# Layer 2 of a decoder on one core: self attention with halves of heads, norms in steps, and an MLP in a written order

## The chip, the cores and the metric

The kernel runs on one core of a Trainium2 chip. A core has a matrix engine (PE, whose weight loads the profile shows as PEld), a vector engine (DVE), an activation engine (ACT), a general engine (POOL), and SP, whose queue starts DMAs. Data lies in SBUF (128 partitions); matmuls write to PSUM, eight banks of 128 x 512 float32. The metric is device time of one execution in microseconds, lower is better; the figure given for the kernel is the median of five.

## The reference, cut to what matters

x is 8 sequences of 112 tokens of width 256 (the functions carry other default sizes; the shapes of the inputs rule). Twelve sublayers follow each other, each added to x. The change is in two of them, the first two of layer 2:

```
x = x + L2_attn(layernorm(x))
x = x + L2_xattn(layernorm(x), ctx_512)

L2_attn:   q = h @ Wq (8 heads of 128), k, v = h @ Wk, h @ Wv (4 heads of 128, each for two q heads)
           q, k = q*cos + rotate_half(q)*sin, the same for k     # rotate_half: (-second half, first half)
           softmax(q k^T / sqrt(128) with a causal mask) @ v, heads side by side, @ Wo
L2_xattn:  x = ln(xx; ln1);  x = x + mha(x, x; a1)               # causal mask after the softmax
           x = ln(x; ln2);   return x + mha(x, ctx; a2)
  mha(x, y): o = softmax(q k^T / sqrt(32)) v, 16 heads of 32, of ln(x), ln(y)
             x_out = x + o @ li1 + b;  return x_out + gelu(ln(x_out) @ li2 + b) @ li3 + b
```

The context ctx_512 has 375 tokens of width 128 for each sequence.

## The kernel before, in words

All is float32 unless said. x stays in SBUF as [token, sequence, width]. T = 896 tokens are worked on in two halves of HT = 448 (four sequences each). Weights come in blobs of up to 1 MB through a ring of eight tiles (`_Ring`, L330 to L352): SP loads the next blob when `done` says that a tile is dead. The program is written through a framework that finds dependences, allocates tiles (a pool's tag with bufs buffers; a new pool takes the space of a closed one, so its tiles wait for the old ones) and orders the instructions of each engine by trace order and readiness. Inside `manual_schedule` PE, DVE and ACT keep the written order among that region's instructions; where they fall among others stays free.

`normalise` (L451) takes `stats` (L433: bn_stats and bn_aggr of each sequence, L440, L441), `rsqrt` (L413: ten small DVE instructions, L418 to L430) and one DVE instruction a sequence (L454). `turned` (L473) transposes four sequences of 128 columns on PE (L477). `mm` (L407) issues matmuls at L410; `cp` (L399) copies in turn on DVE (L403) and ACT (L405); `add_to_x` adds at L493.

`l2_attn` (L1472) has no written order. For each half it makes eight q chunks and four k chunks of 128 rows (two matmuls of 448 columns, which the profile counts as two instructions each), with the rotation of L1496 (two products on 64 partitions that cross over), L1499 (product with cos) and L1500 (sum, on POOL). Then, for each sequence: v (`value`, one matmul group of 512 columns), and for two groups of four heads scores, `softmax_rows` (mask added L503, maximum L505, subtraction L506, exponential L507), `row_sums` (L1527, L1528), `heads_T` (e transposed, L515), the product with v and its scaling (L1518); `out_T` (L539) turns o, and eight matmuls with wo and an add follow.

`l2_xattn` (L1553) opens x1 and xo. `a1_attend` (L1583) first does norm 1 of half 0 (`affine_norm`, L1531: normalise with a second rsqrt, times gain plus bias at L1538 and L1539, odd sequences on POOL, then normalise into xn), turns it (L1546 applies gain and bias), makes q and k of half 0, then norm 1 of half 1; a written loop over the sequences follows: scores, their maxima (L960), q of half 1, denominators and result of earlier ones, the turned maxima nT (L966, copied on DVE at L1631), k of half 1, exponent (L1642, L1649, L1656; the mask product mT on POOL, L1658), product with v of the sequence before (L977), `value` of the next. `query_key`, `value` and `result` share one PSUM bank, "mm". L1671 is a reciprocal, L1676 the scaled copy oT, L1581 the add to xo.

Then a POOL DMA fetches the context (cx, L1564, rows of 512 bytes from the order [sequence and chunk, 125 tokens]). `mha_mlp` (L1742), without a written order, norms xo, and for each half computes eight chunks of the hidden layer (gelu at L1759), calls `ctx_norm` (L1708: in step 0 the norm of 24 context chunks, in step 1 their turns, L1720, and evictions to yT, L1723), and then the output (L1766 bias on POOL, L1767 add). x1 is added (L1567), and `a2_attend` calls the shared `cross` (from L1098): keys and values of sequence 0 from yT (L1135, L1145), norm 2 and turns of half 0, queries (L1156), norm 2 and turns of half 1, and a written loop (maxima L1174, exponentials L1180, turns L1187).

The first layer's `l0_attend` (from L678) is in the form that the change gives to `l2_attn`: a mask matmul in bfloat16 (L739), scores over 64 rows (L746), negated maxima (L755), exponentials with accumulated sums (L761), division before the turn (L769, L770), turns (L778, L780) and a product that comes out transposed (L786, L792).

The functions that the change touches:

Of the kernel before, what the change touches and what calls it, by code (L numbers as in the profile page):

```python
# [12 lines left out]

# [95 lines left out]

def _down(w):  # L110

    return w.transpose(0, 2, 1).reshape(-1, D)


def _weights(inp):
# [75 lines left out]
    def heads(w):  # L191
# [3 lines left out]
        [("l2a_wq", _fm(a("Wq")))],  # L195
        [("l2a_wk", _fm(a("Wk"))), ("l2a_wv", _fm(a("Wv")))],
# [64 lines left out]
def _constants():  # L261
# [12 lines left out]
    for r in range(16):  # L274
# [10 lines left out]
        ("sin", np.concatenate([sin, -sin])),  # L285
# [21 lines left out]
def _pack(inp):  # L307
# [7 lines left out]
        "in_ctx": np.ascontiguousarray(inp["ctx_512"].reshape(NB * CTX, DC)),  # L315
# [8 lines left out]


# [30 lines left out]
class _Kernel:  # L356
# [56 lines left out]
    def rsqrt(self, var, rows, n):  # L413

        nc, small = self.nc, self.small
        va, r0, w, p, rs = (self.t(small, [P, 24], tag)[:rows, :n] for tag in ("va", "r0", "rw", "rp", "rs"))
        vec = nc.vector
# [4 lines left out]
        vec.tensor_scalar(r0.bitcast(I32), r0.bitcast(I32), -1.0, float(0x5F300000), ALU.mult, ALU.add)  # L422
        root = 0.446405130**0.5
        vec.scalar_tensor_tensor(w, r0, root, va, ALU.mult, ALU.mult)
        vec.tensor_tensor(w, w, r0, ALU.mult)
        vec.scalar_tensor_tensor(p, w, -1.38883461 / root, w, ALU.add, ALU.mult)
        vec.scalar_tensor_tensor(p, p, 1.94247540, r0, ALU.add, ALU.mult)
        vec.scalar_tensor_tensor(w, p, -0.5, va, ALU.mult, ALU.mult)
        vec.tensor_tensor(w, w, p, ALU.mult)
        vec.scalar_tensor_tensor(rs, w, 1.5, p, ALU.add, ALU.mult)  # L430
        return rs

    def stats(self, src, rows, n, twice=False):  # L433
# [5 lines left out]
        for i in range(n):  # L439
            nc.vector.bn_stats(st[:rows, i, :], src[:rows, i, :])  # L440
            nc.vector.bn_aggr(mv[:rows, i, :], st[:rows, i, :])  # L441
        var = mv[:rows, :n, 1]
        rs = self.rsqrt(var, rows, n)
        if twice:
            v2 = self.t(small, [P, 24], "v2")[:rows, :n]
            nc.vector.tensor_tensor(v2, rs, rs, ALU.mult)
            nc.vector.tensor_tensor(v2, v2, var, ALU.mult)
            nc.vector.tensor_tensor(rs, rs, self.rsqrt(v2, rows, n), ALU.mult)
        return mv, rs

    def normalise(self, src, dst, rows=S, n=NB, twice=False):  # L451
        mv, rs = self.stats(src, rows, n, twice)
        for i in range(n):
# [3 lines left out]
            )  # L457

# [6 lines left out]
    def ln_T(self, ps, half=None, tag="tr"):  # L465

        for h in (0, 1) if half is None else (half,):
            bs = slice(h * HB, (h + 1) * HB)
            self.normalise(self.x[:, bs, :], self.xn[:, bs, :], n=HB)
# [26 lines left out]
    def softmax_rows(self, sc, work, heads, scale, mask=None):  # L496

        nc = self.nc
        e = self.t(work, [P, 4, S], "e")[:S, :heads, :]
        mx = self.t(self.small, [P, 4], "mx")[:S, :heads]  # L500
        src = sc
        if mask is not None:
            nc.vector.tensor_tensor(e, sc, mask[:, None, :].to_broadcast([S, heads, S]), ALU.add)  # L503
            src = e
        nc.vector.tensor_reduce(mx, src, AX.X, ALU.max)  # L505
        nc.vector.tensor_tensor(e, src, mx[:, :, None].to_broadcast([S, heads, S]), ALU.subtract)  # L506
        nc.scalar.activation(e, e, AF.Exp, scale=scale)  # L507
        return e

    def heads_T(self, e, work, ps, heads, mask=None):  # L510

        nc = self.nc
        tp = self.t(ps, [P, 512], "tr")
        for j in range(heads):
            nc.tensor.transpose(tp[:S, j * S : (j + 1) * S], e[:, j, :], self.ident[:S, :S])  # L515
        eT = self.t(work, [P, 4, S], "eT")[:S, :heads, :]
        src = tp[:S, : heads * S].rearrange("p (h s) -> p h s", h=heads)
        if mask is None:
            self.cp(eT, src)
        else:  # L520
            nc.vector.tensor_tensor(eT, src, mask[:, None, :].to_broadcast([S, heads, S]), ALU.mult)
        return eT

    def scores(self, ps, qk):
        sc = self.t(ps, [P, 512], "sc")
        for j, (q, k) in enumerate(qk):
            self.mm(sc[:S, j * S : (j + 1) * S], [(q, k)])
        return sc[:S, : len(qk) * S].rearrange("p (h t) -> p h t", h=len(qk))

    def out_T(self, o, work, ps, cols):  # L530

        n = cols // P
        oT = self.t(work, [P, n, S], "oT")
        for c0 in range(0, n, 4):
            m = min(4, n - c0)
            tp = self.t(ps, [P, 512], "tr")
            for j in range(m):
                c = c0 + j
                self.nc.tensor.transpose(  # L539
                    tp[:, j * S : (j + 1) * S], o[:S, c * P : (c + 1) * P], self.ident[:S, :S]  # L540
                )
            self.cp(oT[:, c0 : c0 + m, :], tp[:, : m * S].rearrange("p (c s) -> p c s", c=m))
        return [oT[:, c, :] for c in range(n)]

# [5 lines left out]

    def self_psum(self, ctx):
        return ctx.enter_context(self.tc.tile_pool(name="ps_self", bufs=2, space=PSUM))
# [24 lines left out]
    def ln_T_mm(self, ps, xs):  # L577

        self.normalise(self.x, self.xn)
# [258 lines left out]

    def divided(self, out, av, hd, factor=None):

        nc = self.nc
        n = out.shape[1]
        ri = self.t(self.small, [P, 16], "ri")[:S, :n]
        nc.vector.reciprocal(ri, av[:, :, hd])
        if factor is not None:
            nc.vector.tensor_scalar(ri, ri, factor, None, ALU.mult)
        nc.vector.tensor_tensor(
# [735 lines left out]
    def a1_attend(self, x1, xo, norm):  # L1583
# [9 lines left out]
        with ExitStack() as ctx:  # L1593
# [96 lines left out]
            with tc.manual_schedule(engines={ET.PE, ET.DVE, ET.Activation}):  # L1690
                for b in range(NB):
# [8 lines left out]
                    if b < 4:  # L1700
                        query_key(1, b, 1)
# [533 lines left out]
```

## Time and profile before

| | us |
|---|---|
| median of five runs | 2420.91 |
| the five runs | 2410.22, 2420.80, 2420.91, 2421.53, 2426.51 |
| the profiled execution | 2410.22 |
| its span, first to last instruction | 2408.4 |
| PE, DVE, ACT, POOL busy | 2133.7, 1430.3, 772.9, 216.2 |
| self attention of layer 2, from the last add of the sublayer before to its own last add | 1149.5 to 1295.4 |
| a1: prologue; written loop to the score of sequence 7; to the MLP's first turn | 1295.4; 1322.0; 1409.8 to 1447.2 |
| a1's MLP, to its last matmul; to the first maximum of a2 | 1447.2 to 1509.7; 1531.5 |

Times in a profile run from the span's start. A line of a timeline gives start and duration in us, the engine, the source line, the operation, out<-in with partitions x elements, a count, and in square brackets how long the engine had stood still before it and what ended that. A matmul of float32 counts as two instructions. PEclk is the clock that PE was granted, 1.00 being full.

### The profile page before, as it was taken

How to read it: one execution, taken by the hardware profiler on the slowest of the kernel's cores; microseconds unless marked ns; L12 is line 12 of the kernel's file. 1: busy time of each engine (PE TensorE's matmuls, PEld its weight loads, DVE VectorE, ACT ScalarE, POOL GpSimd, SP SyncE). 2: the span in 40 equal slices, each digit the busy share in tenths (PEclk: the TensorE clock that was granted, in tenths of full speed). 3: DMA queues.
4: the chain of work that ended last, by engine and by line, in shares of the span. 5: the costliest groups of instructions: out<-in, count | busy, mean ns of one | idle time of the engine just before them, and what ended most of it. 6: DMA issues, size and time to landing. Idle time of an engine off the chain costs nothing.

```text
span 2408.4 us, 43235 instructions
## 1 busy us (share of the span) xinstructions
PE 2133.7 (89%) x17032; PEld 1266.6 (53%) x17032; DVE 1430.3 (59%) x3994; ACT 772.9 (32%) x2157; POOL 216.2 (9%) x415
## 2 busy tenths in 40 slices
PE   6999999889898899899898859899999999899944
PEld 3444444455556566546565536466655556556622
DVE  4665566565545567553888557767740123667787
ACT  2333334443211256430111211466321110246522
POOL 0111111000011100000222331100000000100000
PEclk9999999999999999999999989999999999899966
DMA  4000000000100000100001011000111100000000
GB/s 187 2 2 2 2 20 35 30 18 18 53 1 15 19 1 2 36 9 35 36 19 35 19 27 53 19 1 4 68 35 53 52 0 1 1 1 2 2 0 16
DMA packets 10731, 55.94 MB, mean 23 GB/s; under 512 B 1834, under 2 KB 3626, under 8 KB 5793
## 3 DMA queue, kind: packets, MB, share of 16 engines
q1 hardware_dynamic: 8304, 44.57, 5.2%
q0 software_dynamic: 2080, 7.07, 0.9%
q8 instruction: 135, 2.21, 0.4%
q10 hardware_dynamic: 144, 1.54, 0.2%
q14 instruction: 68, 0.55, 0.1%
HBM read 52.23 MB, written 0.92 MB: 22 GB/s over the span
## 4 chain that ended last, share of the span: by engine, by line
PE 67%; DVE 21%; issue 5%; ACT 4%; DMA 1%; POOL 1%; DVEq 0%; ACTq 0%; POOLq 0%
PE mm L410 31%; PE gu L410 6%; PE tr L1187 6%; PE g L649 6%; PE sc L410 4%; PE av L1203 3%; PE tr L410 1%; DVE rot L1496 1%; ACT sg L660 1%; PE av L786 1%; PE av L410 1%; ACT th L671 1%; DVE hT L675 1%; PE s L410 1%; PE g L627 1%
## 5 line engine op out<-in xcount | busy, mean ns | idle before, releaser
L649 PE MATMUL g<-w,hT 128*32 128x256 f32 x3552 | 237.3, 384 | 26.1 <-DVE hT L675 25.9
L1174 DVE TENSOR_REDUCE xnm<-sc 112x1 f32<-112x375 f32 x384 | 184.6, 540 | 28.6 <-PE sc L410 28.0
L1187 PEld LDWEIGHTS tr<-cst,xe 112*125 112x125 f32 x1152 | 151.5, 188 | 94.8 <-issue 37.8
L1187 PE MATMUL tr<-cst,xe 112*125 112x112 f32 x1152 | 192.9, 289 | 7.2 <-DVE xeT L1195 4.3
L410 PE MATMUL mm<-xnT,w 128*128 128x448 f32 x432 | 182.3, 559 | 18.8 <-DVE qT L1499 5.3
L410 PE MATMUL mm<-hT,w 128*128 128x448 f32 x512 | 193.0, 539 | 0.0
L649 PEld LDWEIGHTS g<-w,hT 128*32 128x32 f32 x3552 | 95.4, 109 | 168.1 <-DVE hT L675 124.9
L410 PEld LDWEIGHTS mm<-hT,w 128*128 128x128 f32 x512 | 97.1, 190 | 94.4 <-issue 94.4
L627 PE MATMUL g<-xw,cst 128*32 128x256 f32 x1792 | 138.0, 379 | 0.0
L1195 DVE COPY xeT<-tr 125x336 f32<-125x336 f32 x192 | 97.2, 506 | 67.7 <-PE tr L1187 60.8
L1193 ACT COPY xeT<-tr 125x336 f32<-125x336 f32 x192 | 85.0, 443 | 160.2 <-PE tr L1187 160.2
L410 PEld LDWEIGHTS mm<-xnT,w 128*128 128x128 f32 x432 | 77.8, 192 | 104.0 <-issue 54.0
L1178 ACT ACTIVATE xe<-sc,xnm 112x375 f32<-112x375 f32 x256 | 126.2, 581 | 11.2 <-DVE xnm L1174 11.2
L410 PE MATMUL mm<-w,hT 128*112 128x256 f32 x576 | 129.0, 383 | 0.0
L410 PE MATMUL gu<-xnT,w 128*128 128x448 f32 x320 | 126.1, 549 | 1.6 <-DVE hT L1341 1.2
L410 PE MATMUL mm<-w,oT 128*112 128x256 f32 x416 | 105.8, 405 | 22.2 <-DVE oT L1676 13.8
L410 PEld LDWEIGHTS mm<-w,hT 128*112 128x112 f32 x576 | 102.0, 179 | 25.3 <-issue 3.5
L660 ACT ACTIVATE sg<-g 128x192 f32<-128x192 f32 x224 | 73.9, 330 | 105.3 <-PE g L649 92.8
L671 ACT ACTIVATE th<-cell 128x64 f32<-128x64 f32 x224 | 57.5, 257 | 147.3 <-DVE cell L669 147.0
L410 PEld LDWEIGHTS mm<-w,oT 128*112 128x112 f32 x416 | 74.2, 186 | 52.2 <-DVE oT L1676 15.1
L2089 DVE COPY wq<-tr 128x256 bf16<-128x256 bf16 (+1 forms) x12 | 4.6, 420 | 162.9 <-PE tr L2088 162.9
L673 DVE TENSOR_TENSOR h<-sg,th 128x64 f32<-128x64 f32 x224 | 50.4, 225 | 85.6 <-ACT th L671 85.6
(402 smaller groups left out, 3622.2 us busy)
## 6 DMA issues: line engine op xcount, KB each, us to landing
w<-in_w SPq DMA_DIRECT2D x33, 1024.0 KB, 4.8
raw<-in_wq POOLq DMA_DIRECT2D x3, 1024.0 KB, 5.1
w<-in_w SPq DMA_DIRECT2D x3, 896.0 KB, 6.6
wi<-in_wint POOLq DMA_DIRECT2D x3, 768.0 KB, 6.1
w<-in_w SPq DMA_DIRECT2D x2, 768.0 KB, 4.2
ctxT<-in_ctxT ACTq DMA_DIRECT2D x1, 1500.0 KB, 8.3
cx<-in_ctx POOLq DMA_DIRECT2D x1, 1500.0 KB, 20.9
w<-in_w SPq DMA_DIRECT2D x2, 512.0 KB, 3.5
```

The source lines that it names most:

```text
L410: self.nc.tensor.matmul(out, lhsT, rhs, start=i == 0, stop=i == len(pairs) - 1)
L627: nc.tensor.matmul(g[32 * j : 32 * j + 32, :], pick[:, t % 16, :], xw[:, l, t // 16, 256 * j : 256 * j + 256], start=True, stop=t == 0, sk ...
L649: nc.tensor.matmul(g[32 * j : 32 * j + 32, :], hT[l][:, c, :], whh[l][:, c, 256 * j : 256 * j + 256], start=False, stop=c == 1, skip_group ...
L660: nc.scalar.activation(sg[:, :192], g[:, :192], AF.Sigmoid)
L671: nc.scalar.activation(th, cell[l], AF.Tanh)
L673: nc.vector.tensor_tensor(h, og, th, ALU.mult)
L1174: nc.vector.tensor_reduce(nm, sc, AX.X, ALU.max, negate=True)
L1178: nc.scalar.activation(e, sc, AF.Exp, bias=nm)
L1187: nc.tensor.transpose(tp[:CH, i * S : (i + 1) * S], e[:, i * CH : (i + 1) * CH], self.ident[:S, :S])
L1193: nc.scalar.copy(eT, src)
L1195: nc.vector.tensor_copy(eT, src)
L1203: nc.tensor.matmul(avs[b][32 * j : 32 * j + 32, c * S : (c + 1) * S], values[b % 2][:CH, i, 4 * c + j, :], eTs[b, c, j][:, i, :], start=i ...
```

## The change

Self attention takes the form of `l0_attend`. The columns of Wq and Wk are packed so that one chunk of 128 rows holds the first halves of two heads and the next chunk their second halves; a rotation is then six full DVE instructions for two chunks, without POOL, and a head's score is two matmuls over 64 rows. Half 1's norm and rotation, and norm 1 of half 0 for the next sublayer, run as generators, a step at a time, in a written order. In `a1_attend` nT's copy goes to ACT, `value` moves ahead of `exponent`, and the MLP's norm of half 0 is stepped in. The MLP gets a written order of its own (`a1_mlp`), with the context's norm and turns and then norm 2 of half 0 as one chain of steps. The context is packed in the order of its tile and fetched by SP. All generators elsewhere are drained at once.

```diff
@@ _rotary (for Wq and Wk), the packed inputs
+    a = w.reshape(w.shape[0], 2, 2, n // 4, 2, 64)
+    return a.transpose(0, 1, 3, 4, 2, 5).reshape(w.shape)
-        "in_ctx": np.ascontiguousarray(inp["ctx_512"].reshape(NB * CTX, DC)),
+        "in_ctx": np.ascontiguousarray(inp["ctx_512"].reshape(NB * NCH, CH, DC).swapaxes(0, 1)),
...
@@ l2_attn
+            def pair(half, l, i):
+                cols = slice(half * HT, (half + 1) * HT)
+                out, m = ((kT, wk), (qT, wq))[l]
+                cos, sin = turns[l]
+                parts = []
+                for x in range(2):
+                    pm = self.t(ps, [P, 512], "tr")[:, :HT]
+                    c = slice((2 * i + x) * P, (2 * i + x + 1) * P)
+                    self.mm(pm, [(m[:, k, c], self.xnT[:, k, cols]) for k in range(2)])
+                    parts.append(pm.rearrange("p (b s) -> p b s", b=HB))
...
+                nc.vector.tensor_tensor(a, parts[0], cos, ALU.mult)
+                nc.vector.tensor_tensor(rb, parts[0], sin, ALU.mult)
+                nc.vector.tensor_tensor(ra, parts[1], sin, ALU.mult)
+                nc.vector.tensor_tensor(b, parts[1], cos, ALU.mult)
+                nc.vector.tensor_tensor(a, a, ra, ALU.subtract)
+                nc.vector.tensor_tensor(b, b, rb, ALU.add)
+            def prepare(half):
+                for p in range(2):
+                    pair(half, 0, p)
+                    yield
+                    for i in range(2):
+                        pair(half, 1, 2 * p + i)
+                        yield
+            def norm(half):
+                bs = slice(half * HB, (half + 1) * HB)
+                mv, rs = drain(self.stats(self.x[:, bs, :], S, HB))
+                yield
...
+                yield
+                for kc in range(2):
+                    nc.scalar.copy(
+                        self.xnT[:, kc, half * HT : (half + 1) * HT], self.turned(self.xn, ps, kc, half)
+                    )
+                yield
+            def score(b, p):
...
+                    nc.tensor.matmul(
+                        scs[b, p, r].rearrange("p h t -> p (h t)"), ident, mask.rearrange("p h t -> p (h t)"),
+                        start=True, stop=False, skip_group_check=True,
+                    )
+                for i in range(2):
+                    for x in range(2):
+                        for r in range(2):
+                            rows = slice(64 * r, 64 * r + 64)
+                            nc.tensor.matmul(
+                                scs[b, p, r][:, i, :], qT[rows, 2 * p + i, x, cols], kT[rows, p, x, cols],
+                                start=False, stop=x == 1, skip_group_check=True,
+                            )
...
+            with tc.manual_schedule(engines={ET.PE, ET.DVE, ET.Activation}):
+                for _ in norm(0):
+                    pass
+                now = prepare(0)
+                later = chain(norm(1), prepare(1))
+                following = self.norm1(0)
+                for b in range(NB + 2):
+                    on, last = b < NB, 0 < b <= NB
+                    for p in range(2):
+                        if b == 0:
+                            for _ in range(3):
+                                next(now)
+                        if on:
+                            score(b, p)
+                            maxima(b, p)
+                        if last:
+                            turn(b - 1, p)
+                        if on:
+                            exponent(b, p)
+                        if p == 0:
+                            if b > 1:
+                                result(b - 2)
+                        elif on:
+                            value(b)
+                        next(later, None)
+                        if last:
+                            attend(b - 1, p)
+                        if on:
+                            divide(b, p)
+                        if b > 4:
+                            for _ in range(3 if b < NB else 5):
+                                next(following, None)
+                drain(following)
@@ l2_xattn
-                nc.gpsimd.dma_start(cx[:CH], self.args["in_ctx"].rearrange("(n p) d -> p n d", p=CH))
-                self.mha_mlp("a1", xo, lambda ps, half: self.ctx_norm(cx, yT, ps, half))
-            for b in range(NB):
-                nc.vector.tensor_tensor(xo[:S, b, :], xo[:S, b, :], x1[:S, b, :], ALU.add)
+                nc.sync.dma_start(cx[:CH], self.args["in_ctx"])
+                self.a1_mlp(xo, lambda ps: self.ctx_norm(cx, yT, ps))
@@ a1_attend
-                nc.vector.tensor_copy(nTs[b], tp)
+                nc.scalar.copy(nTs[b], tp)
...
+            following = self.normalise(xo[:, :HB, :], self.xn[:, :HB, :], n=HB)
...
                         query_key(1, b, 1)
+                    if b + 1 < NB:
+                        value(b + 1)
                     exponent(b)
+                    if b > 5:
+                        for _ in range(4):
+                            next(following, None)
                     if b > 0:
                         attend(b - 1)
-                    if b + 1 < NB:
-                        value(b + 1)
@@ norm2, a1_mlp, mlp_hidden, mlp_out
+    def norm2(self, half):
+        for b in range(half * HB, (half + 1) * HB):
+            self.nc.vector.tensor_tensor(self.xo[:S, b, :], self.xo[:S, b, :], self.x1[:S, b, :], ALU.add)
+            yield
+        yield from self.affine_norm(self.xo, self.x1, self.w("l2x_ln2_g"), self.w("l2x_ln2_b"), half)
...
+            with tc.manual_schedule(engines={ET.PE, ET.DVE, ET.Activation}):
+                self.transposed(self.xn, ps, evac, (0,))
+                between = self.normalise(xo[:, HB:, :], self.xn[:, HB:, :], n=HB)
+                for _ in self.mlp_hidden("a1", ps, hTs[0], 0):
+                    next(between, None)
+                drain(between)
+                self.transposed(self.xn, ps, evac, (1,))
+                between = chain(context(ps), self.norm2(0))
+                for _ in self.mlp_out("a1", ps, hTs[0], 0, xo):
+                    next(between, None)
+                for _ in self.mlp_hidden("a1", ps, hTs[1], 1):
+                    for _ in range(3):
+                        next(between, None)
+                for _ in self.mlp_out("a1", ps, hTs[1], 1, xo):
+                    for _ in range(4):
+                        next(between, None)
+                for _ in between:
+                    pass
```

`mlp_hidden` and `mlp_out` are the two loops of `mha_mlp` with a yield after each chunk (eight) and each sequence (four). In `l2_attn`, `turn` is four transposes and an ACT copy, `exponent` four exponentials with accumulated sums, `attend` two matmuls and a copy (DVE for p 0, ACT for p 1), `divide` a reciprocal and a product on DVE. `rsqrt` yields after three, three and four instructions, `stats` after each sequence, the end of `normalise` after every two. `ctx_norm` yields through its norm (39 steps) and after each of its eight turns.

## The prediction

> **What bounds the kernel now.** I read the page's busy shares first. TensorE (PE) is busy 89% of the span, and the PE line of the 40 slices shows a clock of 9 tenths nearly everywhere, so time is won only where PE stands still or its clock is down. Then I asked for the busy time of each engine in the stretches of this block. Columns: stretch, length, then busy time (and instructions) of PE, PEld, DVE, ACT, POOL, then PE clock, DMA share, GB/s.
>
> ```profile
> 1149.50:1174.00 24.50, 20.65 (x60) 9.10 (x61) 22.94 (x48) 2.35 (x3) 10.19 (x9) 1.00 0.15 62
> ...
> 1179.70:1222.00 42.30, 40.19 (x258) 32.56 (x259) 31.77 (x67) 9.90 (x18) 0.00 (x0) 1.00 0.00 1
> 1222.00:1246.90 24.90, 22.44 (x60) 9.63 (x59) 23.82 (x44) 0.00 (x0) 12.48 (x12) 1.00 0.12 43
> ...
> 1428.10:1442.20 14.10, 0.97 (x22) 0.56 (x14) 0.37 (x2) 0.00 (x0) 0.00 (x0) 0.51 0.33 92
> ...
> 1509.90:1536.00 26.10, 20.33 (x54) 8.10 (x54) 20.96 (x62) 5.05 (x11) 6.67 (x8) 0.87 0.11 41
> ```
>
> Rows 1 and 3 are the rotary stretches of the two halves (VectorE, DVE, 94% busy), row 2 is four batches of self attention (PE 95% busy), row 4 is empty, and row 5, the way into the second attention, is 80% DVE. The timeline says why row 4 is empty: DVE's queue holds statistics of the context tile cx ahead of the last attention's product, and cx has not landed.
>
> ```profile
> 1420.85 3.56 POOL L1564 DMA_DIRECT2D cx<-in_ctx  x1
> ...
> 1424.44 3.31 POOL L1658 TENSOR_TENSOR mT<-eT,cst 112x448 f32<-112x448 f32 x3
> ...
> 1441.83 0.49 DVE L440 BATCH_NORM_STATS2 st<-cx 125x6 f32<-125x128 f32 x2 [15.71 <-DMA cx<-in_ctx]
> 1442.23 0.61 DVE L1676 TENSOR_TENSOR oT<-av,rd 128x448 f32<-128x448 f32 x1
> ...
> 1442.90 3.76 PE L410 MATMUL mm<-w,oT 128*112 128x256 f32 x8 [13.82 <-DVE oT L1676]
> ```
>
> PE waits 13.82 us, and its next eight instructions take 3.76 us where the same eight took 1.98 at 1422.10: the clock had fallen. POOL's issue also sat 3.56 us between the first mT and the other three.
>
> **1. Layer 2's self attention (1149.5 to 1295.4, 145.9 us).** Rotary, before, per chunk: three DVE products of 0.62 us and a POOL sum of 1.13 us. After, per pair of chunks: four products from PSUM and two sums, six DVE instructions at the 0.64 us spacing of L1496 and L1499, 3.85 us. So DVE pays the same 1.93 us a chunk and POOL's sums go, which nothing but the stretch's last one waited for (1.13 us). PE needs eight instructions of 0.375 us, 3.0 us a pair.
>
> A batch on PE, before: value 1.72, scores 1.8, e turned 0.8, products 1.8, o turned 0.8, result 3.4; sum 10.3, and values follow each other every 10.17 us (1191.41, 1201.58). After, by the rows of the first layer's attention, which has the same form: two masks and sixteen half-row score instructions 0.33 + 0.97 us a half batch (there 511.17 to 512.65 with masks twice as wide), four turns 0.5, two products of 224 columns at 1.2 columns a ns in four instructions 0.75, and per batch value 1.72 and result 3.4. Sum 2 x 2.55 + 5.1 = 10.2. Turning o goes, masks come: **a batch costs PE the same**. DVE falls from some 7.5 to 4.2 us a batch (four half-size maxima 1.2, two divisions 1.6, a copy 0.62, an add 0.42; the exponent's accumulator replaces the sums), ACT rises to 5.0; neither binds.
>
> So only the second half's 24.9 us rotary stretch can gain: its 18 us of PE work moves between batches 1 to 4, where DVE has room (batches 2 and 3: PE 10.2 + 6.0, DVE 4.2 + 7.7). Against it, statistics of half 1 (4.6 us) and its normalising (1.4) now stand in DVE's written order inside the first, DVE-bound prologue. Walk: tokens turned at 1149.5 as before (PSUM comes free then); first pair's product 1153; DVE 23.1 (six pairs) + 4.6 + 1.4 + 1.3 + 1.6, with waits, to 1187; batch 1 with pair and turns 13; batches 2 and 3 16.2 each; batch 4 13.2 + 2 (its second score waits for the last pair); 5 to 7 30.6; tail 11.6 (two half batches and two results). End 1290: **-5 us**. What is late next is PE itself. The next norm's DVE steps (0.6 us each, three a half batch) fit beside it, as they did before. Range -15 (prologue overlapped better) to +8 (1 us more a batch).
>
> **2. The cross block's self attention (1295.4 to 1409.8).** Its prologue keeps its 26.6 us: norm 1 of half 0 was already done by 1294.7. In the loop:
>
> ```profile
> 1373.74 2.95 DVE L1671 RECIPROCAL rd<-su 128x448 f32<-128x448 f32 x1
> ...
> 1376.61 0.36 DVE L1581 TENSOR_TENSOR xo<-mm,xo 112x256 f32<-112x256 f32 x1
> 1376.88 0.61 DVE L1631 COPY nT<-tr 128x448 f32<-128x448 f32 x1
> ...
> 1377.55 1.85 PE L1642 MATMUL s<-nT,cst 1*112 1x448 f32 x8 [2.78 <-DVE nT L1631]
> ```
>
> Moving nT's copy to ACT should free PE at 1375.4 (turn's end 1374.8 and a 0.53 us copy), but value(b+1) now comes first, and it waits for the one "mm" bank that the add (1376.97) frees; the exponent's and the product's matmuls queue behind it. So 0.5 us a batch of the 2.78 goes; for the first four batches value waits 0.75 us for kT's copy out of the same bank, a loss. Clock drops after these waits (periods 14.5, 13.2 against 11.6) may get rarer. Together **-1 us**, -7 to +3.
>
> **3. Tail and context load (score of batch 7 at 1409.8 to the MLP's first turn at 1447.2: 37.4 us).** New: exponent at +4.9 (no nT queue, no value), exponentials from +6.4, four masks on POOL without the DMA to +11.5, product +12.9, oT +13.6, result +15.7, add: 16.1. **-21 us**, the surest term. cx goes through SP, contiguous by partition. Issued when the attention's tiles come free (about 9 us before the MLP), it is first read some 19 us into the MLP. Its landing lies between 8.3 us (ctxT, 1500 KB, ACT queue) and the 20.9 of today; SP has no later load ahead of it. Hidden by 7 us even at the long end.
>
> The Trainium skill (DMA: Bandwidth & Descriptors, "Why a DMA increments its semaphore by 16 and not by 1") says a transfer uses the largest number of engines up to 16 that divides its slowest dimension; for 125 partitions that is five, on SP as well. Row 4's share of 0.33 of 16 engines agrees; at its 92 GB/s the load would take 17 us, still hidden.
>
> **4. The MLP (1447.2 to its last product, 1509.7: 62.5 us).** New: 1.9 to the first product, 12 (1478.16 to 1490.2) + 0.6 for the table load, turn 1.0, out 13.7 (1464.35 to 1478), hidden 12, out 13.7 with one context turn 0.6: 55.5. **-7 us**: the low clock of 1442 to 1452 (0.77 in that stretch) and the wait of 2.4 us at 1494 go.
>
> **5. The way into the second attention (1509.7 to its first maximum, 1531.48: 21.8 us).** Here the written order costs. Before, norm 2 of half 0 filled DVE's gaps in the MLP.
>
> ```profile
> 1479.35 0.43 DVE L440 BATCH_NORM_STATS2 st<-xo 112x6 f32<-112x256 f32 x1
> ...
> 1492.27 1.38 DVE L454 TENSOR_SCALAR xn<-x,mv,rs 112x256 f32<-112x256 f32 x4
> ...
> 1531.48 0.53 DVE L1174 TENSOR_REDUCE xnm<-sc 112x1 f32<-112x375 f32 x1
> ```
>
> These 14.3 us plus sums and statistics of three batches (3 x 1.1) are 17 us of DVE. After, the chain is context first (24 + 3 + 12 + 8 = 47 steps), norm 2 behind it, and the MLP takes 4 + 24 + 16 = 44 steps. So three context turns and all of norm 2 are left when PE is done. DVE then: add and seven yT evictions 5.1, norm 2 of half 0 17, of half 1 13.6 (three batches' part fits in MLP gaps), evictions, values and queries 7.1: 42.8 instead of 21.8. PE's keys, values and queries, paced by DVE before too, hide inside, and the two queries that stood between the first maximum and the steady loop are done: -2.5. **+18.5 us**, +8 to +22.
>
> A rule speaks against such a tail: the skill (TensorE: Matmul & The Clock Gate, "Part 1: The HAM clock gate") halves PE's clock after an idle window of about 3.4 us until PE was busy as long. The 3.76 us row agrees. By the rule the restart adds about 1.7 us; without it nothing, since DVE sets the pace there.
>
> **Sum**: -5 - 1 - 21 - 7 + 18.5 = -15.5 us on the profiled execution's 2410.2 (span 2408.4). That was the fastest of five; the median is 2420.9, so the forecast is 2405.4, **2405**. The split of norms into steps changes no instruction elsewhere; 0 us.
>
> **Rivals.** (a) *Slower: the round trip of a half batch binds.* A turn's copy, the product and its copy follow each other in written order; in the first layer's attention PE idles 0.9 and 0.7 us a half there, and a batch takes 13.70 us with PE busy 11.98. If the new loop ran at 13.7 instead of 10.2, +3.5 x 8 = 28, net +12.5: 2433. Against: result and value stand in that gap, 3.4 and 1.7 us against a 0.75 us copy. It decides at 12.1 us a batch. (b) *Norm 2 hides*: norm 2 of half 1 put behind the first scores (-13.6 of the +18.5): -29, 2392. Against: before, the first maximum came right after half 1's eviction (1531.48). (c) *The context still comes late* (SP held, cx after its first use): 12 us back, -3.5: 2417.
>
> **Chances.** Forecast (-6 to -24, 2397 to 2415) 0.45, (b) and better 0.25, (c) or no gain to speak of 0.2, (a) 0.1. Two in ten lie beyond 2383 (the good ends of 1, 2 and 5 taken in part) and 2425. About 0.5%, 12 us, is what a measurement can tell from no change: of the forecast 0.29 lies beyond it, with (b) 0.54 faster; 0.06 slower ((a) beyond); 0.40 the same.
>
> **What would show it.** Right: no wait of DVE on cx; four mT in one run of 4.4 us; batches 5 to 7 of the new attention 10.2 us apart; after the MLP's last product some 17 us of norm 2 on DVE with PE idle, then norm 2 of half 1, first maximum about 43 us after it. Wrong: a period over 12 us, maxima waiting on divisions, or PE busy behind the MLP.

## The result, and the profile after

The changed kernel takes 2422.2 us (median of 34 runs, 2416.8 to 2428.1) where the kernel before, run beside it, takes 2420.3: the ratio, taken round by round, is **1.0012, 95% interval 1.0005 to 1.0019**, 2.9 us slower (the two medians lie 1.9 us apart). By the prediction's own bound of 0.5% that is no difference; it had forecast 15.5 us less. The profiled execution of after has a span of 2419.3 us.

Much was changed, and the sum is next to nothing, so the first question is where a gain went. Two executions can't be laid over each other by the clock: the turn of the tokens that opens the changed part starts at 1149.5 us in before and at 1155.2 in after, and in the twelve experiments anywhere from 1149.7 to 1164.6, though the code ahead of it is the same in all. So I measure stages, from one PE event to the next:

| stage (us) | before | after | predicted change | measured |
|---|---|---|---|---|
| tokens turned to score of sequence 1 of the cross block | 181.1 | 175.4 | -5 | -5.7 |
| score of sequence 1 to score of sequence 7 | 79.2 | 92.8 | -1 | **+13.6** |
| score of 7 to the MLP's first turn | 37.4 | 21.6 | -21 | -15.7 |
| the MLP, first turn to last product's end | 62.5 | 55.4 | -7 | -7.1 |
| from there to the first turn of the second attention's loop | 26.4 | 44.4 | +18.5 | +18.0 |
| sum | 386.6 | 389.6 | -15.5 | +2.9 |

That the stages of one execution add up to the 2.9 us of the runs is partly chance: in e3 and e4 below the second stage took 89.7 us, 3 less than in after, though e4 leaves its code as it is. Three rows are within 1 us of their forecast and the third misses by 5 us; the second misses by 14.6 us, which alone turns the sign. (The prediction's step 1 ends, and its step 2 begins, with the last add of the self attention, inside the first row. Between these ends step 1 is -8.4 us, 145.9 to 137.4, and step 2, up to the score of sequence 7, is +16.3, 114.4 to 130.7: 1.3 in its prologue, 1.4 in sequence 0, 13.6 in the second row.)

The rows of after that answer to the stretches shown of before; columns as there (stretch, length, busy time and instructions of PE, PEld, DVE, ACT, POOL, clock, DMA share, GB/s).

```profile
1155.20:1191.20 36.00, 29.40 (x97) 14.20 (x98) 27.93 (x70) 5.15 (x19) 0.00 (x0) 0.86 0.10 42
...
1245.76:1265.90 20.14, 20.14 (x147) 15.63 (x145) 11.10 (x37) 9.71 (x40) 0.00 (x0) 1.00 0.06 23
1433.00:1445.00 12.00, 8.76 (x55) 4.94 (x52) 7.14 (x9) 0.27 (x1) 7.33 (x8) 0.86 0.30 124
1500.40:1526.60 26.20, 15.88 (x35) 5.30 (x33) 21.41 (x78) 3.17 (x5) 6.22 (x8) 0.60 0.11 40
1526.60:1544.80 18.20, 13.56 (x40) 5.91 (x41) 17.50 (x55) 2.44 (x8) 6.33 (x8) 0.83 0.00 0
```

Row 1 is the way into the new self attention, DVE busy 27.9 of 36.0 us. Row 2 is two sequences of it, from value to value: 20.14 us, PE busy for all of it, 10.07 each (the prediction said 10.2). Row 3 is the end of the cross block's attention, no longer empty. Rows 4 and 5 are the way into the second attention: DVE at 82% and 96%, PE's clock at 0.60 and 0.83.

Now the stage that failed. One late sequence of the cross block's loop in after, PE, DVE and ACT, from nT's copy to the next score; the bracket is the idle time of the engine before the instruction, and who ended it.

```profile
1402.03 0.53 ACT L1731 COPY nT<-tr 128x448 f32<-128x448 f32 x1 [4.36 <-PE tr L926]
1403.61 0.36 DVE L1681 TENSOR_TENSOR xo<-mm,xo 112x256 f32<-112x256 f32 x1
...
1404.03 1.97 PE L428 MATMUL mm<-w,ynT 128*112 128x512 f32 x4 [2.09 <-DVE xo L1681]
...
1405.93 1.02 PE L1742 MATMUL s<-nT,cst 1*112 1x448 f32 x8
...
1406.77 0.96 PE L1749 MATMUL s<-qT,kT 32*112 32x112 f32 x32
...
1407.67 0.97 PE L937 MATMUL av<-mT,vb 112*32 112x112 f32 x32
...
1408.79 0.62 DVE L1776 TENSOR_TENSOR oT<-av,rd 128x448 f32<-128x448 f32 x1 [4.81 <-PE av L937]
1408.84 0.58 ACT L1721 COPY vb<-mm 112x512 f32<-112x512 f32 x1 [6.28 <-PE av L937]
1409.32 1.85 ACT L1756 ACTIVATE eT<-s 112x448 f32<-112x448 f32 x4
1409.92 2.33 PE L428 MATMUL s<-kT,qT 32*112 32x112 f32 x32 [1.28 <-ACT eT L1756]
```

nT is ready at 1402.6, but value stands ahead of the exponent on PE and waits 2.09 us for the mm bank: that wait the prediction had named. It had not followed value's *copy*. On ACT the copy of vb (L1721) stands ahead of the exponentials, and it waits for PE's attend (L937), 6.28 us idle: attend(b-1) still reads one of the two vb buffers. So the exponentials start 2.55 us after the matmuls of their input (1406.77), where 1.04 is enough in e8 below, and the next score, which needs their PSUM banks, waits 1.28 us and is then paced by them (2.33 us where 32 scores take 1.05 in before).

### The profile page after: what moved, and what is told of

Read it like the earlier page. It is cut to its first block, busy times and chain, and to the rows that moved or that the text cites. A ratio compares the mean times of both kernels' runs of the same rounds, so it can differ in the third digit from the quotient of the medians.

```text
span 2419.3 us, 43350 instructions
## 1 busy us (share of the span) xinstructions
PE 2155.4 (89%) x17064; PEld 1273.8 (53%) x17064; DVE 1387.7 (57%) x3944; ACT 796.7 (33%) x2291; POOL 185.0 (8%) x390
## 4 chain that ended last, share of the span: by engine, by line
PE 70%; DVE 18%; ACT 5%; issue 4%; POOL 1%; DMA 1%; DVEq 0%; ACTq 0%; POOLq 0%
PE mm L428 33%; PE tr L1147 6%; PE g L621 6%; PE gu L428 6%; PE sc L428 4%; PE av L1163 3%; PE tr L428 3%; PE s L428 1%; ACT sg L632 1%; PE av L758 1%; ACT th L643 1%; DVE hT L647 1%; PE g L599 1%; DVE h L645 1%; DVE cell L641 1%
## 5 line engine op out<-in xcount | busy, mean ns | idle before, releaser
L621 PE MATMUL g<-w,hT 128*32 128x256 f32 x3552 | 237.3, 384 | 26.2 <-DVE hT L647 25.9
L428 PE MATMUL mm<-xnT,w 128*128 128x448 f32 x336 | 144.8, 573 | 12.9 <-DVE qT L1116 4.8
L1155 DVE COPY xeT<-tr 125x336 f32<-125x336 f32 x192 | 97.2, 506 | 67.9 <-PE tr L1147 60.7
L632 ACT ACTIVATE sg<-g 128x192 f32<-128x192 f32 x224 | 73.9, 330 | 104.6 <-PE g L621 92.8
L428 PEld LDWEIGHTS mm<-xnT,w 128*128 128x128 f32 x336 | 63.2, 199 | 77.1 <-issue 44.9
```

Of the source, the lines that this page charges most:

```text
L428: self.nc.tensor.matmul(out, lhsT, rhs, start=i == 0, stop=i == len(pairs) - 1)
L621: nc.tensor.matmul(g[32 * j : 32 * j + 32, :], hT[l][:, c, :], whh[l][:, c, 256 * j : 256 * j + 256], start=False, stop=c == 1, skip_group ...
L632: nc.scalar.activation(sg[:, :192], g[:, :192], AF.Sigmoid)
L1155: nc.vector.tensor_copy(eT, src)
```

## The experiments

Ratios are to the kernel before, run beside each; five rounds each. "After" stands at 1.0012.

### First set: what costs in the loop, and what in the way

The theory at this point was the vb buffer. Its rivals were the move of nT's copy to ACT, and the mm bank with the clock that falls behind waits.

**e1_three_values**

```diff
+            third = ctx.enter_context(tc.tile_pool(name="a1_v", bufs=1))
...
-                vbs[b] = self.t(work, [P, 16, 32], "vb")
+                vbs[b] = self.t(third if b % 3 == 2 else work, [P, 16, 32], "vb")
...
-                nTs[b] = self.t(work, [P, 4, S], "nT")
+                nTs[b] = self.t(acts, [P, 4, S], "nT")
```

> The changed kernel with a third buffer for the value tile vb of the cross block's self attention (nT gives up its second one, SBUF holds no more). Theory (the copy of value b+1 waits for the product of b-1, because two buffers hold three live values, and the exponentials stand behind it): the loop from its first maxima to the last score goes from 102.2 us back to 85 to 88, no score waits for an exponential, the kernel gains 13 to 17 us (about 2406). Rival one (the copy of nT on ScalarE is what costs): under 2 us. Rival two (value's waits for the one mm bank and the clock that drops behind them): those waits stay, so under 4 us.

**e2_value_back**

```diff
-                    if b + 1 < NB:
-                        value(b + 1)
                     exponent(b)
...
                     if b > 0:
                         attend(b - 1)
+                    if b + 1 < NB:
+                        value(b + 1)
```

> The changed kernel with value(b+1) put back behind attend(b-1), nT's copy still on ScalarE. Theory: two values are alive at most, so the loop is back at 85 to 89 us and the kernel 12 to 16 us faster; if it is as fast as with three buffers, moving value ahead is worth nothing by itself. Rival one (nT's copy on ScalarE): the loop stays above 99 us. Rival two (mm bank): as the theory in total, but then the third buffer alone does not recover it.

**e3_shift_on_dve**: `nc.vector.tensor_copy(nTs[b], tp)` in place of `nc.scalar.copy(nTs[b], tp)`.

> The changed kernel with the copy of nT back on VectorE, value still ahead of exponent. Theory: the loop stays at 100 to 106 us and the kernel within -2 to +4 us, since the wait for vb's buffer is untouched. Rival one: the loop falls below 92 us and the kernel gains 10 us or more.

Measured: e1 2413.7 us, 0.9988 (0.9974 to 1.0002), its loop stage 84.6 us. e2 **2391.9 us, 0.9894 (0.9878 to 0.9911)**, loop 65.1 us. e3 2420.6 us, 1.0007 (0.9993 to 1.0021), loop 89.7 us.

The nT rival is out: with the copy on DVE the kernel is as slow as after, within the intervals. But my theory was hit as well. The third buffer gave back about 6 of the 14 us (0.24%; nT, which had to give up its second buffer for it, still waited for nothing but its turn, in all eight sequences), and putting value back gave 28 us against after, twice what had to be explained. Two windows of e1, each one sequence long, tell half of the story:

```profile
1398.98:1413.63 14.65, 12.56 (x132) 7.71 (x128) 5.99 (x7) 2.83 (x7) 4.29 (x5) 0.74 0.01 1
1413.63:1425.00 11.37, 9.28 (x132) 5.79 (x128) 7.98 (x15) 2.35 (x6) 3.81 (x5) 1.00 0.01 1
```

At full clock the sequence takes 11.37 us, 2.1 less than the 13.43 of the same sequence in after: the buffer's share, as the theory had it. Four of the six sequences of e1's stage, however, ran 14.65 to 15.06 us: two that also hold queries and keys (13.26 in e8 below), and two at a clock of 0.74 and 0.80. And even 11.37 is more than e2's 9.45. So the buffer is one part only, and the place of value ahead of the exponent costs by itself. That is the second theory, tried below with e8.

**e4_norm2_earlier**

```diff
+                later = chain(context(ps), self.norm2(0))
                 for _ in self.mlp_hidden("a1", ps, hTs[0], 0):
                     next(between, None)
+                    next(later, None)
...
-                between = chain(context(ps), self.norm2(0))
+                between = later
                 for _ in self.mlp_out("a1", ps, hTs[0], 0, xo):
-                    next(between, None)
+                    for _ in range(6):
+                        next(between, None)
```

> The changed kernel with the context's statistics begun one step earlier in the MLP (beside the hidden layer of half 0) and six of its steps, not one, behind each output product of half 0, so that all of the context and of norm 2 of half 0 is issued before the MLP's last product. Theory (VectorE's backlog of context turns and norm 2 sets the way into the second attention): from the last MLP product to the first turn of the second attention 44.4 us becomes 24 to 30, the MLP stays at 55 to 59 us, the kernel gains 12 to 19 us. Rival (VectorE has no room left in the MLP, 45 us of work by rows in some 55): the MLP grows by what the way loses, and the kernel gains under 4 us.

Measured: 2416.2 us, 0.9996 (0.9981 to 1.0012), about 4 us better than after, where the theory had 12 to 19. The way falls from 44.4 to 34.0 us, and the MLP grows from 55.4 to 60.7. Each side had half of it: DVE's backlog does set the way, and the MLP has no room for all of it. What is left of the way is seen in e6.

### Second set: one part alone

**e5_context_only**: the kernel before with `in_ctx` packed by partition and `nc.sync.dma_start(cx[:CH], self.args["in_ctx"])`.

> The kernel before with the context load alone changed (packed by partition, through SP's queue). Theory: DVE no longer stands 15.7 us on cx and POOL no longer issues 3.56 us between two masks, so the score of sequence 7 to the MLP's first turn falls from 37.4 us to 18 to 22 and the kernel gains 14 to 18 us (2399 to 2403). Rival (the load is late on SP as well): under 6 us.

**e7_shift_alone**: the kernel before with `nc.scalar.copy(nTs[b], tp)`.

> The kernel before with the copy of nT alone moved from VectorE to ScalarE, value still behind attend. Theory now (PE's 2.8 us wait a batch was the copy's place behind the reciprocal and the add in VectorE's queue, and value's move gave it back): seven scores of the loop take 64 to 68 us instead of 79.2, the kernel gains 11 to 15 us. Rival (the copy was worth the 0.5 us a batch of the prediction): 1 to 4 us.

**e8_value_between**

```diff
-                    if b + 1 < NB:
-                        value(b + 1)
                     exponent(b)
+                    if b + 1 < NB:
+                        value(b + 1)
```

> The changed kernel with value(b+1) between exponent(b) and attend(b-1): still ahead of attend, so three values share two buffers, but no longer ahead of the exponent, and its copy stands behind the exponentials on ScalarE. Theory now (the place ahead of the exponent costs: the wait for the mm bank, the copy ahead of the exponentials, and nothing left to fill PE's time behind them): seven scores take 65 to 70 us instead of 92.8, the kernel gains 22 to 28 us on the changed one (2393 to 2398). Rival (the wait for the buffer itself costs): over 78 us, and under 15 us of gain.

**e10_good_parts**: the kernel before with the new `l2_attn`, the copy of nT on ACT and the context load of e5.

> The kernel before with the three parts that should pay alone: the new layer 2 self attention (with norm 1 of half 0 in steps), the copy of nT on ScalarE, the context load on SP; value's place and the whole MLP as before. Theory: the gains add, -7 -13 -16, minus 33 to 40 us, 2377 to 2384, and the way into the second attention stays at 20 to 24 us. Rival (they share one wait, as the tail of the attention follows the loop's last product): under 28 us.

**e8 decides**: 2393.6 us, 0.9897 (0.9884 to 0.9909), loop 65.1 us, the same as e2. Value still runs ahead of attend, three values still share two buffers; only its place against the exponent is other. One late sequence of e8, PE, DVE and ACT:

```profile
1373.73 1.05 PE L428 MATMUL s<-kT,qT 32*112 32x112 f32 x32
...
1373.92 0.59 ACT L1721 COPY vb<-mm 112x512 f32<-112x512 f32 x1 [1.01 <-PE av L937]
...
1378.06 0.53 ACT L1731 COPY nT<-tr 128x448 f32<-128x448 f32 x1 [3.55 <-PE tr L926]
...
1378.64 1.02 PE L1742 MATMUL s<-nT,cst 1*112 1x448 f32 x8 [0.68 <-ACT nT L1731]
...
1379.48 0.96 PE L1749 MATMUL s<-qT,kT 32*112 32x112 f32 x32
...
1380.38 1.97 PE L428 MATMUL mm<-w,ynT 128*112 128x512 f32 x4
1380.52 1.84 ACT L1756 ACTIVATE eT<-s 112x448 f32<-112x448 f32 x4 [1.94 <-PE s L1749]
...
1382.28 0.97 PE L937 MATMUL av<-mT,vb 112*32 112x112 f32 x32
...
1383.18 0.36 PE L428 MATMUL s<-kT,qT 32*112 32x112 f32 x4
```

The copy of vb still waits for attend, but behind the exponentials, where no one is in a hurry for ACT. Value's 1.97 us fill the time in which ACT works on the exponentials, the mm bank has been freed by then (the add ends at 1380.16), and the score follows attend without a wait. PE's only wait in 9.45 us is 0.68 us for nT. The difference to the 13.50 us of after, term by term: value's wait 2.09 in place of the 0.68, +1.41; the score's wait, +1.28; its slower pace, 2.33 against 1.05, +1.28. Sum +3.97, measured +4.05. The last sequence of e1 parts the two terms of the score: with the third buffer the score waits for nothing at its start and runs 1.55 us, so that 2.06 of the 2.56 us were the copy's wait for its buffer, and 0.5 stay.

e7: 2402.6 us, 0.9939 (0.9925 to 0.9954), loop 66.1 us instead of 79.2. The copy of nT was worth 13 us, not the half microsecond a batch of the prediction: PE's wait before the exponent falls from 2.78 to 0.68 us.

```profile
1391.09 1.02 PE L1642 MATMUL s<-nT,cst 1*112 1x448 f32 x8 [0.68 <-ACT nT L1631]
```

With the long wait gone the clock stays up (sequences 4 and 5 of the loop took 14.5 and 13.2 us in before, at 0.77 and 0.87, and 9.46 now). So the change did hold this gain, and value's move hid it: 66 us as it could be, 79 before, 93 after.

e5: 2411.1 us, 0.9967 (0.9953 to 0.9981), 8 us where 14 to 18 were expected. Score of 7 to the MLP takes 27.4 us, 10 less than before. In its timeline (SP's queue, then DVE):

```profile
1427.98 0.34 SPq L1564 DMA_DIRECT2D cx<-in_ctx  x1
...
1443.97 0.49 DVE L440 BATCH_NORM_STATS2 st<-cx 125x6 f32<-125x128 f32 x2 [8.79 <-DMA cx<-in_ctx]
...
1445.40 0.41 DVE L1581 TENSOR_TENSOR xo<-mm,xo 112x256 f32<-112x256 f32 x1
1445.87 1.75 PE L477 MATMUL tr<-cst,xn 112*128 112x112 f32 x8 [9.20 <-DVE xo L1581]
```

The load still takes 16.0 us from issue to first use (21.0 in before, from POOL; on SP, too, some five of the 16 engines are at work, a DMA share of 0.29 from 1428.30 to 1436.60), and the attention's last add (L1581) still stands behind the context's statistics. The new queue and packing give 5 us of loading and free POOL between the masks, 10 us of the 15.7 that this stage gains in after. Another 2.2 are nT's (35.1 us in e7), and e10 below, which has both, takes 25.2. Only the last 3.5 us, to after's 21.6, are left for the written order, which lets DVE reach the context when the MLP is well under way: in after cx is first read 33 us after its issue, without a wait.

e10: 2388.2 us, 0.9876 (0.9863 to 0.9888), 30 us, short of the expected 33 to 40, as the load gave 8 and not 16. The gains do add: 7.0 (e9, below), 14.8 (e7) and 8.0 (e5) are 29.8. The way stays at 23.9 us, since the MLP is in its old order.

### Third set: the whole, the self attention alone, and norm 2

**e6_both**: e2 and e4 together.

> The changed kernel with value back behind attend and with the context and norm 2 of half 0 begun earlier in the MLP. Theory (the two losses lie in stages of their own): the gains add, -25 and -3 to -5 on the kernel before, 2385 to 2391; the tail takes 21 us, the MLP 60, the way into the second attention 34. Rival (with the loop repaired the MLP's pieces meet another state of the queues): no better than value back alone, 2391 to 2396.

**e9_self_attention_only**: the kernel before with the new `l2_attn` and norm 1 of half 0 in its steps.

> The kernel before with the new layer 2 self attention alone (norm 1 of half 0 in steps beside it); the cross block as before. Theory: -5 to -8 us, as the stage's 173.0 us fell to 165.9 in the trace of the changed kernel, which is 2410 to 2413. Rival (the stage's gain comes with a colder prologue behind it, or is drift): within 2 us of before.

**e11_both_norm2_in_loop**: e6 with norm 2 of half 1 inside the second attention's loop; **e12_parts_norm2_in_loop**: the same on e10.

```diff
-        qsrc(ps, 1)
+        later = qsrc(ps, 1)
...
+                for _ in range(4):
+                    next(later, None)
-                if c == 3 and b < 2:
-                    query(1, 2 * b)
-                    query(1, 2 * b + 1)
+                if c == 3 and first <= b < first + 2:
+                    query(1, 2 * (b - first))
+                    query(1, 2 * (b - first) + 1)
```

> The kernel e6_both with norm 2 of half 1 and its two turns taken out of the way into the second attention and put in steps, four a step, behind the first seven steps of its loop; the queries of half 1 move one sequence later. Theory (VectorE's backlog sets the way): the way falls from about 34 to 20 to 24 us and the loop's first two sequences lose 0 to 5, so 7 to 13 us better than e6_both. Rival (VectorE is as full in the loop): under 3 us better.

> The kernel e10_good_parts (the MLP in its old order) with the same move of norm 2 of half 1 into the loop. Theory: the way falls from 23.9 to 14 to 17 us and the kernel gains 4 to 9 us on e10_good_parts, 2379 to 2384, the fastest of all. Rival: the loop's first sequences give all of it back, under 2 us.

Measured: **e6 2387.9 us, 0.9864 (0.9840 to 0.9888)**, the largest gain of all, 33 us below before, with e10 (0.9876) inside its interval. Its stages are 174.0, 65.1, 20.7, 62.7 and 34.4. e9 2413.3 us, 0.9971 (0.9954 to 0.9989): 7 us, where 5 to 8 were expected (in its trace the new self attention takes 137.4 us, as in after, and one sequence of the loop behind it, at a clock of 0.76, loses 2.8 us again). e11 2395.9 us, 0.9892 (0.9871 to 0.9914) and e12 2393.0 us, 0.9886 (0.9865 to 0.9908): no better than the kernels they start from, rather worse. The first two stretches of the second attention's loop, up to about the result of sequence 0, e6 ahead of e11:

```profile
1506.59:1529.00 22.41, 21.69 (x202) 12.85 (x202) 15.41 (x31) 14.69 (x47) 0.07 (x1) 1.00 0.01 2
1529.00:1551.50 22.50, 20.89 (x177) 12.12 (x176) 15.25 (x30) 14.38 (x45) 0.54 (x1) 1.00 0.00 1
```

```profile
1507.68:1530.00 22.32, 21.10 (x199) 12.27 (x197) 20.14 (x56) 14.35 (x47) 2.69 (x4) 1.00 0.01 1
1530.00:1560.00 30.00, 23.09 (x179) 13.24 (x178) 22.98 (x62) 14.36 (x45) 5.44 (x6) 0.94 0.00 1
```

DVE has 7 us free in e6's first row and 2 in e11's, and PE is at its limit in e6 (21.7 of 22.4 us). The loss shows in the second rows: PE stands idle for 6.9 us of 30.0 in e11 and for 1.6 of 22.5 in e6. That norm 2's instructions come between a maximum and the copy of a turned tile, and so delay PE, is my reading; no run shows which of them does it. In e11 the way falls by 7.1 us; the result of sequence 0 comes 53.0 us after the loop's first turn instead of 45.0, and sequence 1 follows after 25.6 us instead of 20.7. The loop gives back 12.9 us for 7.1.

## Why the prediction was wrong

**Step 2 failed**, "Together -1 us, -7 to +3": it is +16.3. The reading of the profile behind it was right as far as it went. Value does wait for the one mm bank, and of the 2.78 us wait 0.69 go (2.09 are left). Two costs were put at nothing. First, the step followed value's matmuls on PE but not its copy on ACT: I asked what is queued behind the waiting instruction on PE, and did not ask it of the copy, which has the exponentials behind it and a buffer before it that only attend frees. That is 2.06 us a sequence at full clock, the part that e1's third buffer gives back. Second, I counted what the moved instruction meets in its new place and not what it leaves in the old one: behind the exponent, value had been PE's work while ACT ran the exponentials (e8's lines show it there). Without it the score is paced by the exponentials, 0.5 us. Together 2.56 us: the last sequence of the stage, 11.56 us in before, should come to 11.56 - 0.69 + 2.56 = 13.43, and it measures 13.43. With both, and with the clock that falls behind longer waits (0.77 to 0.91 in three of after's six sequences of the stage), the loop takes 92.8 us instead of 79.2. The range of that step had reached to +3 only.

The same step also under-read the gain it held. Of nT's move alone I made nothing, since value stood in its way; e7 puts it at 13 us of the stage and 0.6% of the kernel. Had I costed the two edits apart, the sum would have shown that one of them eats the other.

**Step 1 was right**, and a little better than told: -5 forecast, -8.4 between its own ends and -7.0 in e9's runs; 10.07 us a sequence against 10.2.

**Step 3 was too good by 5 us** (-21, measured -15.7). The exponentials came 1.7 us later than told (8.1 us behind the score, not 6.4), most of it the slow score of step 2 again. Four masks did run in one stretch of 4.4 us, but POOL had been given other work first. After, POOL and PE at the end of the attention:

```profile
1433.28 1.51 POOL L1904 TENSOR_TENSOR xo<-xo,w 112x256 f32<-112x256 f32 x2 [5.50 <-DVE xn L476]
...
1434.75 4.44 POOL L1758 TENSOR_TENSOR mT<-eT,cst 112x448 f32<-112x448 f32 x4
...
1437.02 0.38 PE L937 MATMUL av<-mT,vb 112*32 112x112 f32 x2 [0.54 <-POOL mT L1758]
...
1440.92 3.55 PE L428 MATMUL mm<-w,oT 128*112 128x256 f32 x8 [0.72 <-DVE oT L1776]
```

Two bias sums of the MLP (L1904) stand in POOL's queue ahead of the masks and wait 5.50 us for the MLP's norm of half 0, which the change had stepped into this place. In e5 the masks of sequence 7 begin 0.62 us after the exponentials (1427.81 and 1428.43); here, with the exponentials at 1431.43, that would be 1432.05, and they begin at 1434.75. PE starves between the masks, and its last result runs 3.55 us instead of 1.98. No experiment moved these sums alone, so their price, 2.7 us and the clock behind it, is a reading of the trace.

**Steps 4 and 5 were right in their sums**: -7.1 for -7, +18.0 for +18.5. One sign of step 5 was not met: the first maximum came 36.4 us behind the MLP's last product (1536.75), not 43, ahead of the end of norm 2 of half 1; what that norm held up was the loop's first turn, at 44.4. And PE did not only wait for norm 2: it was busy for 15.9 of the first 26.2 us, and ran at half clock there:

```profile
1514.10 2.07 PE L428 MATMUL mm<-w,yT 128*125 128x512 f32 x2 [0.56 <-ACT xkT L1095]
...
1519.81 2.07 PE L428 MATMUL mm<-w,yT 128*125 128x512 f32 x2 [0.78 <-DVE xv L1105]
1527.11 1.98 PE L501 MATMUL tr<-cst,xn 112*128 112x112 f32 x8 [5.22 <-DVE xn L476]
```

The same two value matmuls take 1.03 us inside the loop, and the eight turns 0.99 at the start of the MLP. The prediction had this restart cost nothing, as DVE sets the pace; but DVE, too, stood 3.0 us behind the first of these values (until 1516.21) and 1.0 behind the last (until 1521.92).

**The rivals.** (a), a slower self attention, did not come: 10.07 us. (b), norm 2 of half 1 behind the first scores, was put at -13.6 us; e11 and e12 built it, and the loop gave back more than the way had won. (c), a late context, did not come either; in e5, where the load is the same and DVE keeps its old order, DVE did wait 8.79 us for it. The rival that came true, a slower loop of the cross block, was not among them, though the prediction had named the clock that drops after PE's waits in that very loop.

## What to carry to other kernels

When an instruction is moved forward on one engine, follow its result to the engine that evicts it, and ask there the same two questions: what does the eviction wait for (the buffer as well as the data), and what stands behind it in that queue. Then look at the hole it leaves: work that filled another engine's time in the old place is missed there. And cost two edits of one loop apart before adding them, since a gain of 13 us and a loss of 28 look like a small change.

## What the runs showed that I had not expected

**The same wait, with and without a loss of clock.** In after the value that waited 2.09 us at 1404.03 ran at full speed, 1.97 us. In e1 the value with the same wait ran 3.05 us, and the next matmuls 1.85 and 1.72 where they take 1.02 and 0.96:

```profile
1405.86 3.05 PE L428 MATMUL mm<-w,ynT 128*112 128x512 f32 x4 [2.09 <-DVE xo L1681]
...
1408.84 1.85 PE L1743 MATMUL s<-nT,cst 1*112 1x448 f32 x8
```

The Trainium skill (TensorE: Matmul & The Clock Gate, "Part 1: The HAM clock gate") has PE's activity watched over a free-running window of about 3.4 us, so that it would matter how a wait lies to the window. The traces agree. Every change of the granted clock in the fourteen of them lies on a grid of 3.41 us. In e1 the wait (1403.77 to 1405.86) lies whole inside one step of that grid, 1403.20 to 1406.61, in which PE is busy for 1.32 us; from 1406.61 the clock is 0.50 for two steps. In after the wait (1401.94 to 1404.03) is parted by the end of a step at 1403.18; PE is busy for 2.17 us of the one step and 2.56 of the next, and the clock stays at 1.00. So a wait well under 3.4 us can be enough, where the prediction had gone by an idle window of about 3.4 us. From 100 us on, in no trace did the full clock outlast a step with more than 1.90 us of idle PE; it also fell behind some with less (1.28 us ahead of 1382.70 in after), so the idle time of a step is not the whole rule. e1's repair was lost to this: 2.1 us a sequence won at full clock, and 3.3 and 3.4 us paid in the two sequences at 0.74 and 0.80.

**DVE beside POOL.** In e6, in the last products of the MLP, DVE first and then POOL at the same time:

```profile
1467.61 0.94 DVE L1655 TENSOR_TENSOR xo<-xo,x 112x256 f32<-112x256 f32 x1
1468.48 0.94 DVE L1626 TENSOR_TENSOR x<-x,w 112x256 f32<-112x256 f32 x1
...
1471.08 0.41 DVE L1626 TENSOR_TENSOR x<-x,w 112x256 f32<-112x256 f32 x1
```

```profile
1467.37 0.90 POOL L1625 TENSOR_TENSOR x<-x,w 112x256 f32<-112x256 f32 x1
1468.35 0.79 POOL L1626 TENSOR_TENSOR x<-x,w 112x256 f32<-112x256 f32 x1
1469.22 1.65 POOL L1680 TENSOR_TENSOR xo<-x,w 112x256 f32<-112x256 f32 x2
```

A DVE sum or product of two SBUF tiles takes 0.94 us while POOL runs one, and 0.41 in POOL's pause. POOL's half of norm 2 is thus not free help. The Trainium skill (GPSIMD Engine Reference, "1. Specifications") names this case, DVE instructions with two SBUF inputs; the rows agree, and give its size here.

**The start of a stage moves by 15 us** between profiled executions of kernels that share all code ahead of it (1149.7 to 1164.6 us). Whole spans of single executions say little about a change of 10 us; stages between two events of one engine, and medians over rounds, say more; a stage, too, differed by 3 us between executions of the same code (92.8 in after and 89.7 in e4).
